# Adapter factors split into float32r parts of 64 rows, and the value bias joined to the output projection's row

## The chip, the cores and the metric

The kernel runs on one core of one Trainium2 chip. The metric is device time in microseconds (us) of one execution. The engines are named as the profile names them: PE is TensorE (matmuls; PEld is its weight load), DVE is VectorE, ACT is ScalarE, POOL is GpSimd, and SP only issues DMA transfers. "Bank" is one PSUM bank of 128 partitions x 512 float32 values, which is what one 128x512 matmul fills.

## The reference

x is float32 of 8 batches x 512 tokens x 512 features. It goes through four sublayers, each followed by a layer norm over the features:

```python
x = layernorm(x + attn0(x))   # 16 heads of 32, causal, biases on Q, K, V, O
x = layernorm(x + moe(x))     # 8 experts, top 2, adapters of rank 16
x = layernorm(x + attn1(x))   # grouped queries, 8 heads on 2
x = layernorm(x + ffn(x))     # SwiGLU on integer weights
```

The change touches the first two:

```python
q, k, v = x @ WQ.T + WQ_b, x @ WK.T + WK_b, x @ WV.T + WV_b     # per head of 32
attn = softmax(causal(q k^T / sqrt(32)))
attn0 = (attn @ v) @ WO.T + WO_b

router = xf @ gate.T + xf @ (2 * B @ A).T ; softmax ; top 2, renormalised
gup = xf @ gate_up[e] + 2 * (xf @ gup_A[e].T) @ gup_B[e].T      # 512 -> 512, A: 16 x 512
h   = silu(gup[:256]) * gup[256:]
out = h @ down[e] + 2 * (h @ down_A[e].T) @ down_B[e].T         # 256 -> 512, A: 16 x 256
moe = sum over the two chosen experts of weight * out
```

The rows of a softmax sum to 1, so a bias on v passes through the attention unchanged: `attn @ (v + bv) = attn @ v + bv`.

## The kernel before, in words

**Stages.** Attention of layer 0 runs from 0 to about 744 us, the experts to about 1160, attention of layer 1 to about 1750, and the integer feed-forward network to the end at 2309. Attention 0 works through 8 batches of about 94 us. Each batch has 4 groups g of 4 heads, and each group 3 units u of the keys' tiles (tile 0; tiles 1 and 3; tile 2), so there are 12 slots (g, u) to a batch. A slot makes its scores (`sc`, L1256), which ACT turns into `p` by an exponential (L1260) and POOL masks with an affine select (L1265). Then come the slot's other jobs, a list called `todo`, and then the products of the slot before (`av`, L1280), whose `p` VectorE adds up (L1288). In slot (g+1, 1) the group before is normalised: the sums over keys `rs` (L1295), ACT's copy `r_inv` of them, the reciprocal on VectorE (L1298, 3.34 us), and `aoT` (L1299).

**The order.** The block runs under `in_order`, which fixes TensorE's order to that of the text; the instructions of the other engines are placed by a scheduler that respects it. Every engine runs its own queue in order and waits on semaphores. The jobs in a slot are the values of the next batch (`value`, L1185, `ps_v`), the queries and keys of the next group (L1192, L1200), the output projection of the batch before (`project`, L1208), its transposes (`turn`), the router's logits (`score`) and choice (`choose`), and a `merge`.

**The adapters.** The adapters are not applied to tokens; the product of their factors is added to the experts' weights. For each pair of experts and each of 6 column blocks c a `merge` makes two products of 128x512 (`delta`, L749, factors of 16 rows in float32), ACT scales each by 2 into a tile `scaled` (L760) and POOL adds it into the expert's weights (L762). There are 24 merges. Two are done in each of batches 1 to 6, in slots (2, 0) and (3, 0); two stand after batch 7, and ten among the first expert steps. The factors of four experts are loaded by `load_lora` (L744) at the start, those of the other four in batch 7, 16 rows of 1792 values at partitions 0, 32, 64 and 96.

**Rings and banks that tie things together.** All jobs' matmuls use the PSUM tag `mm`, which has two banks; `sc` has one buffer of four banks. The SBUF tag `r_inv` has two buffers, which the normaliser's `r_inv` and the merge's `scaled` take in turn: a new user waits until the last reader of the one before is done, and for `scaled` that is POOL's add (L762), for `r_inv` POOL's add into `g_total` (L934). The `row` tile holds two rows broadcast over the partitions: WV's bias, added to each `ps_v` by VectorE (L1187), and WO's, added by POOL to the whole x of a batch (L1374) ahead of its projection. `first_turned` rooms of the first expert steps reuse the places of `row` and `logits` when attention is done.

**The tail.** When the last batch has gone through, expert steps begin (`tiles.step`: a tile's gate and up matmuls L845, the transposes of the step before, the down matmuls L862, and the fetch and transposes of later rows). Between them stand the last batch's transposes, logits, choice and dispatch, and one merge to a step.

Of the kernel before, what the change touches and what calls it, by code (L numbers as in the profile page):

```python
# [18 lines left out]
P = 128  # L19
NB = 8  # L20
S = 512
# [24 lines left out]
LORA = 3 * 512 + 256  # L46
EXPERT = UPS * 512
# [6 lines left out]
V_BQ, V_BK, V_NS, V_SS, V_SG, V_SU = 0, 4, 8, 12, 16, 16 + NHID  # L54
N_VEC = 16 + 2 * NHID
# [17 lines left out]
class Env:  # L73
# [53 lines left out]
    def load_adapters(self, pool):  # L127
        nc, ins = self.nc, self.ins
        self.lora_sb = pool.tile([P, 2, LORA], F32, name="lora_sb")
        for i in range(2):  # L130
            for j in range(4):
                nc.sync.dma_start(out=self.lora_sb[32 * j : 32 * j + R, i, :], in_=ins.lora[i, j])
        self.wr = pool.tile([P, ND, E], F32, name="wr")
        nc.sync.dma_start(out=self.wr, in_=ins.w_router)
        self.ra = pool.tile([R, D], F32, name="ra")
        nc.sync.dma_start(out=self.ra, in_=ins.router_lora_a)
        self.rb = pool.tile([R, E], F32, name="rb")
        nc.sync.dma_start(out=self.rb, in_=ins.router_lora_b)
# [246 lines left out]
class Router:  # L385
# [4 lines left out]
    def __init__(self, env, keep, pool, small, tmp, dram):  # L390
# [37 lines left out]
        i = tmp.tile([P, 1], I32, name="r_lane_i")  # L428
# [290 lines left out]
class Experts:  # L719
# [20 lines left out]
    def load_lora(self, pool, i):  # L740

        self.lora = pool.tile([P, LORA], F32, tag="lora", name=f"lora_{i}")
        for j in range(4):
            self.nc.sync.dma_start(out=self.lora[32 * j : 32 * j + R, :], in_=self.env.ins.lora[i, j])  # L744

    def delta(self, ps, e, c):
        j = 32 * (e % 4)
        a, bt = lora_factors(self.lora[j : j + R, :], c)
        self.nc.tensor.matmul(ps, lhsT=a, rhs=bt, start=True, stop=True)  # L749
# [15 lines left out]
class Tiles:  # L765
# [115 lines left out]
    def step(self):  # L881
        i = self.next
        self.next += 1
        if i + 1 < self.n:
            self.gate_up(i + 1, lambda: self.turn_hidden(i))
        else:
            self.turn_hidden(i)
        for n in range(4 if i == 0 else 5, 6):
            self.fetch(i + n)
        self.down(i)  # L890
        self.turn_rows(i + 3)
# [222 lines left out]
def attention0(env, guard, keep, routes, experts, dram, p_mm, tiles_ctx):  # L1114
# [8 lines left out]
    with ExitStack() as phase:  # L1123
# [33 lines left out]
        row = work.tile([P, 2, D], F32, name="row")  # L1157
        nc.sync.dma_start(out=row, in_=ins.rows.partition_broadcast(P))
# [9 lines left out]
        experts.load_lora(work, 0)  # L1168
# [13 lines left out]
        def value(b, t):  # L1182
# [4 lines left out]
            nc.vector.tensor_tensor(vs[t], ps, row[:, 0, :], ALU.add)  # L1187
# [122 lines left out]
        def plan(b):  # L1310
# [22 lines left out]
            if b == 0:  # L1333
                todo[1, 0].append(lambda: router.merge_lora(mm([P, ND, E], "ps_wr")))
            if b > 1:
                todo[0, 2].append(lambda: dispatch(b - 2))
                todo[1, 1].append(lambda: enter(one_hot(b - 2, range(NT))))
# [14 lines left out]
        def begin():  # L1352
            pair = work.tile([P, 2, D], F32, tag="row", name="first_turned")
            one = work.tile([P, S], F32, tag="logits", name="first_turned")
            tiles.begin([pair[:, 0, :], pair[:, 1, :], one], work.tile([P, 256], F32, name="first_h"),
# [11 lines left out]
        for b in range(NB):  # L1367
            todo = plan(b)
            for g in range(ND):
                if g == 2:  # L1370
# [3 lines left out]
                    nc.gpsimd.tensor_tensor(xs[b], xs[b], row[:, 1:2, :].to_broadcast([P, NT, D]), ALU.add)  # L1374
                if g == 3 and b + 1 < NB:
                    load_x(b + 1)
                if b == NB - 1 and g == 1:
                    experts.load_lora(work, 1)
# [36 lines left out]
        for c in range(ND):  # L1415
            turn(b, c)
        tiles.step()
# [6 lines left out]
        for places in ((0, 1), (2, 3)):  # L1424
            rows = one_hot(b, places)
            tiles.step()
            merge()
        enter(rows)
        tiles.of_fixed = router.fixed(routes)
        while merges:  # L1430
            tiles.step()
# [519 lines left out]
def _layout(a):  # L1951
# [26 lines left out]
    def columns(n):  # L1978
# [3 lines left out]
                           rows("L0_ffn_down_lora_A")], axis=3)  # L1982
    return {
# [5 lines left out]
                                  "L1_ffn_s_gate", "L1_ffn_s_up")], axis=1),  # L1989
# [29 lines left out]
```

## Time and profile before

| | us |
|---|---|
| median of 4 runs | 2311.31 (2307.61 to 2314.86) |
| the profiled execution | 2316.82 |
| its span | 2315.1 |
| PE busy | 2267.3 |
| DVE / ACT / POOL busy | 1238.9 / 654.2 / 502.1 |
| mean granted clock of TensorE | 0.994 |

The span is the time from the first instruction to the last of the profiled execution. A part of the profile that is used below is the timeline: a line gives the start in us, the duration in us, the engine, the source line and operation, the tiles (out <- in), the shape as partitions x elements, and the number of records that the line joins; in brackets stands the idle time of the engine just before it and what ended that idle time. A float32 matmul of 128x512 leaves two records and a float32r matmul one. A second view gives windows of time: the window, its length, the busy time of TensorE in it with the number of instructions, the clock that the throttle granted (1.00 is full speed), the share of DMA time, and GB/s.

Longest waits of TensorE, in all, from the view of waits (us in total, times, longest):

```
PE sc L1256 <- ACT p L1260: 5.2, 7, 1.8
PE ps_v L1185 <- DVE v L1187: 4.6, 5, 1.4
PE ps_q L1192 <- DMA experts<-in_xT: 4.4, 1, 4.4
PE ps_lora L749 <- DVE first_h L848: 2.9, 1, 2.9
```

The five waits for `v` stand at the start of batches 2 to 6, and the waits of `sc` for `p` behind the merge of slot (2, 0) in batches 1 to 6.

### The profile page before, as it was taken

The page shows a single profiled execution, that of the slowest core. Times are in us where ns is not written, and L with a number is a line of the kernel's source. Part 1 is how long each engine was busy: PE and PEld are TensorE (multiplying, and loading weights), DVE is VectorE, ACT ScalarE, POOL GpSimd, SP SyncE. Part 2 cuts the span into 40 slices and gives each one's busy share as a digit, 9 for nine tenths or more (in the row PEclk, how much of TensorE's full clock was granted, in tenths as well). Part 3 has the DMA queues.
Part 4 walks back from the last instruction along what each step waited for, and adds up shares of the span by engine and source line. Part 5 has one row for each costly group of instructions (what it writes and reads, how often), then busy time and mean ns, then how long its engine had stood idle before and what let it go on. Part 6 is the DMA issues. An engine that isn't in the chain of part 4 may idle for free.

```text
span 2315.1 us, 24139 instructions
## 1 busy us (share of the span) xinstructions
PE 2267.3 (98%) x9430; PEld 1140.8 (49%) x9430; DVE 1238.9 (54%) x1976; ACT 654.2 (28%) x937; POOL 502.1 (22%) x489
## 2 busy tenths in 40 slices
PE   9999999999998999999999999999999999999997
PEld 3344444444443444444543333333333777877776
DVE  3557565666667432232236776667666544444443
ACT  2332332323323221111223333333232222222222
POOL 2231423423324231221123222331211000000000
PEclk9999999999999999999999999999999999999999
DMA  8010110101112243332242011110100100000000
GB/s 286 19 55 1 55 49 7 55 19 37 54 37 87 87 140 124 106 109 91 87 156 63 15 40 55 55 36 19 37 1 1 54 19 19 19 19 19 19 19 20
DMA packets 58443, 126.62 MB, mean 55 GB/s; under 512 B 6210, under 2 KB 6210, under 8 KB 58322
## 3 DMA queue, kind: packets, MB, share of 16 engines
q1 hardware_dynamic: 47040, 89.32, 10.9%
q0 software_dynamic: 10560, 34.61, 5.1%
q8 instruction: 77, 1.26, 0.2%
q10 hardware_dynamic: 722, 1.07, 0.1%
q14 instruction: 44, 0.36, 0.1%
HBM read 89.59 MB, written 35.39 MB: 54 GB/s over the span
## 4 chain that ended last, share of the span: by engine, by line
PE 85%; DVE 8%; issue 2%; DMA 2%; POOL 2%; ACT 1%; POOLq 0%; SPq 0%; DVEq 0%; ACTq 0%
PE ps_gu L845 10%; PE ps_f L1061 7%; PE ps_g L1047 6%; PE ps_u L1047 6%; PE sc L1571 5%; PE av L1591 5%; PE ps_q L1495 5%; PE ps_o L1208 5%; PE ps_y L862 5%; PE ps_o L1543 5%; PE ps_q L1192 4%; PE ps_k L1200 4%; PE ps_v L1185 3%; PE av L1280 3%; PE sc L1256 3%
## 5 line engine op out<-in xcount | busy, mean ns | idle before, releaser
L845 PE MATMUL ps_gu<-experts,xrT 128*128 128x512 f32 (+1 forms) x520 | 247.2, 598 | 0.0
L1260 ACT ACTIVATE p<-sc 128x2048 f32<-128x2048 f32 (+1 forms) x96 | 152.9, 1593 | 189.0 <-PE sc L1256 182.1
L1574 ACT ACTIVATE p<-sc 128x1024 f32<-128x1024 f32 x128 | 131.0, 1024 | 256.2 <-PE sc L1571 243.8
L934 POOL TENSOR_TENSOR g_total<-g_total,r_inv 128x512 f32<-128x512 f32 x64 | 89.7, 1401 | 413.6 <-DVE r_inv L1602 338.2
L1265 POOL TENSOR_SCALAR_AFFINE_SELECT p<-p 128x512 f32<-128x512 f32 x128 | 93.0, 741 | 378.5 <-ACT p L1260 374.9
L1052 DVE SCALAR_TENSOR_TENSOR hT<-ps_u,vec,sg 128x512 f32<-128x512 f32 x88 | 65.9, 748 | 203.5 <-PE ps_u L1047 203.5
L1061 PE MATMUL ps_f<-ffn_w,h_half 128*128 128x512 f32 x672 | 169.7, 393 | 1.2 <-DVE h_half L1056 1.1
L1602 DVE RECIPROCAL r_inv<-r_inv 128x512 f32<-128x512 f32 x32 | 107.3, 3352 | 117.6 <-ACT r_inv L931 117.6
L1288 DVE TENSOR_TENSOR p<-p 128x1536 f32<-128x1536 f32 (+2 forms) x96 | 129.3, 1346 | 41.2 <-POOL p L1265 24.2
L1571 PE MATMUL sc<-qT,kT 64*128 64x512 f32 x512 | 144.2, 641 | 0.7 <-ACT qT L1497 0.7
L1047 PE MATMUL ps_g<-x_high,ffn_w 128*128 128x512 f32 x352 | 141.4, 402 | 3.0 <-DVE x L1549 3.0
L1582 DVE TENSOR_TENSOR p<-p,p 128x1024 f32<-128x1024 f32 x96 | 126.2, 1315 | 28.7 <-PE av L1591 13.9
L1061 PEld LDWEIGHTS ps_f<-ffn_w,h_half 128*128 128x128 f32 x672 | 124.5, 188 | 34.0 <-DVE h_half L1056 7.2
L1047 PE MATMUL ps_g<-x_low,ffn_w 128*128 128x512 f32 x352 | 139.8, 397 | 0.0
L1047 PE MATMUL ps_u<-x_low,ffn_w 128*128 128x512 f32 x352 | 139.5, 396 | 0.0
L1047 PE MATMUL ps_u<-x_high,ffn_w 128*128 128x512 f32 x352 | 139.4, 396 | 0.0
L848 DVE TENSOR_TENSOR h<-ps_gu,h 128x256 f32<-128x256 f32 x67 | 28.4, 423 | 206.5 <-ACT h L847 206.5
L1591 PE MATMUL av<-p,v 128*64 128x512 f32 x512 | 138.0, 617 | 0.2 <-ACT p L1574 0.2
L862 PE MATMUL ps_y<-experts,hT 128*128 128x512 f32 (+1 forms) x272 | 127.9, 592 | 0.5 <-ACT hT L856 0.5
L1192 PE MATMUL ps_q<-experts 128*128 128x512 f32 x256 | 120.2, 611 | 4.4 <-DMA experts<-in_xT 4.4
L845 PEld LDWEIGHTS ps_gu<-experts,xrT 128*128 128x128 f32 x520 | 89.1, 191 | 67.7 <-issue 67.7
L1185 PE MATMUL ps_v<-experts 128*128 128x512 f32 x256 | 116.3, 602 | 4.6 <-DVE v L1187 4.6
(255 smaller groups left out, 3517.2 us busy)
## 6 DMA issues: line engine op xcount, KB each, us to landing
results<-y SPq DMA_DIRECT2D x68, 256.0 KB, 2.0
x<-in_x SPq DMA_DIRECT2D x8, 1024.0 KB, 8.0
experts<-in_gate_up SPq DMA_DIRECT2D x8, 1024.0 KB, 11.8
rows<-x SPq DMA_DIRECT2D x32, 256.0 KB, 2.0
x<-rows SPq DMA_DIRECT2D x8, 1024.0 KB, 11.1
experts<-in_xT SPq DMA_DIRECT2D x7, 1024.0 KB, 5.4
out<-x SPq DMA_DIRECT2D x28, 256.0 KB, 2.3
ffn_i<-in_wq_ffn SPq DMA_DIRECT2D x11, 512.0 KB, 4.2
```

The lines of the kernel that those rows point to most:

```text
L845: mm = nc.tensor.matmul(ps, lhsT=xT[:, c, :], rhs=self.weights(i, c), start=c == 0, stop=c == ND - 1)
L862: self.nc.tensor.matmul(ps, lhsT=hT[:, c, :], rhs=self.weights(i, ND + c), start=c == 0, stop=c == self.NI - 1)
L1047: nc.tensor.matmul(ps, lhsT=w[:, ts(dc, P)], rhs=x[:, dc, :], start=(dc, i) == (0, 0), stop=(dc, i) == (ND - 1, 1))
L1061: self.nc.tensor.matmul(os[t], lhsT=h[:, ts(t, P)], rhs=self.weights(2 * NHID + c), start=(c, i) == (0, 0), stop=(c, i) == (NHID - 1, 1))
L1185: nc.tensor.matmul(ps, lhsT=xts[b][:, c, ts(t, P)], rhs=wv[:, c, :], start=c == 0, stop=c == ND - 1)
L1192: nc.tensor.matmul(ps, lhsT=wq[:, g, ts(c, P)], rhs=xts[b][:, c, :], start=c == 0, stop=c == ND - 1)
L1260: nc.scalar.activation(p, sc[:, :, :width], AF.Exp, scale=scale)
L1288: nc.vector.tensor_tensor(total[:, :, P * kt :], total[:, :, P * kt :], p[:, :, at : at + w], ALU.add)
L1571: nc.tensor.matmul(sc[:, j, :], lhsT=st["kT"][hs, ts(kt, P)], rhs=st["qT"][g][hs, :], start=True, stop=True)
L1574: nc.scalar.activation(p, sc, AF.Exp, scale=scale)
L1582: nc.vector.tensor_tensor(total, total, p, ALU.add)
L1591: nc.tensor.matmul(st["av"][HD * j : HD * (j + 1), :], lhsT=st["v"][:, kt, HD * j : HD * (j + 1)], rhs=p[:, j, :], start=kt == 0, stop=kt ...
```

## The change

Adapters. On the host each factor row is repeated: a pair of experts has 128 rows, 64 for each expert, which are its 16 rows four times over. The kernel fetches a pair in four parts of 512, 512, 512 and 256 columns into one tile `l_raw`, and splits each part. `l_high` is the raw value rounded to float32r, with its sign turned in some of the four copies. `lora` is `raw * low + high` with `low` 0 or 1, which is the rounded value in one set of copies and what rounding leaves of it in the other. The two factors of a product have these copies in different order, so that the sum over 64 rows holds high x high, high x low, low x high and low x low, and one float32r matmul of 64 rows stands for the float32 matmul of 16.

```diff
+    def masks(self, pool, lane):
+        bits = pool.tile([P, 2], I32, name="l_bits")
+        self.low = pool.tile([P, 2], F32, name="l_low")
+        self.sign = pool.tile([P, 2], F32, name="l_sign")
+        for i, bit in enumerate((2 * R, R)):
+            nc.vector.tensor_scalar(bits[:, i : i + 1], lane, bit, None, ALU.bitwise_and)
+        nc.vector.tensor_copy(self.low, bits)
+        nc.vector.tensor_scalar(self.low, self.low, 1.0, None, ALU.min)
+        nc.vector.tensor_scalar(self.sign, self.low, -2.0, 1.0, ALU.mult, ALU.add)
+        self.parts = [(q, c) for q in range(E // 2) for c in range(LORA_PARTS)]
+
+    def fetch_part(self, pool):
+        if self.parts:
+            q, c = self.parts[0]
+            at, n = 512 * c, min(512, LORA - 512 * c)
+            self.raw = pool.tile([P, 512], F32, tag="raw", name="l_raw")
+            self.nc.sync.dma_start(out=self.raw[:, :n], in_=self.env.ins.lora[q, :, at : at + n])
+
+    def split_part(self, pool):
+        q, c = self.parts.pop(0)
+        if c == 0:
+            self.lora = pool.tile([P, LORA], F32R, tag="lora", name=f"lora_{q}")
+        at, n = 512 * c, min(512, LORA - 512 * c)
+        i = int(c in (1, 2))
+        high = pool.tile([P, 512], F32R, tag="r_inv", name="l_high", bufs=2)[:, :n]
+        nc.scalar.activation(high, self.raw[:, :n], AF.Copy, scale=self.sign[:, i : i + 1])
+        nc.vector.scalar_tensor_tensor(self.lora[:, at : at + n], self.raw[:, :n], self.low[:, i : i + 1],
+                                       high.bitcast(F32), ALU.mult, ALU.add)
+        if (q, c) != (E // 2 - 2, LORA_PARTS - 1):
+            self.fetch_part(pool)

     def delta(self, ps, e, c):
-        j = 32 * (e % 4)
-        a, bt = lora_factors(self.lora[j : j + R, :], c)
+        j = P // 2 * (e % 2)
+        a, bt = lora_factors(self.lora[j : j + P // 2, :], c)
         self.nc.tensor.matmul(ps, lhsT=a, rhs=bt, start=True, stop=True)
```

The sixteen splits are placed in slots: four in batch 0, two each in batches 3, 4, 6 and 7, and four among the expert steps. The next part is fetched as soon as a split is issued, and needs the one `raw` buffer, so it waits for that split. `load_lora` at the start and in batch 7 falls away. In the tail two merges move from the steps between the one-hot rows to the last steps, which take two merges each.

```diff
+            slots = {0: ((2, 0), (2, 2), (3, 0), (3, 2)), 3: ((3, 1), (3, 2)), 4: ((1, 1), (1, 2)),
+                     6: ((3, 1), (3, 2)), 7: ((0, 1), (1, 1))}
+            for slot in slots.get(b, ()):
+                todo[slot].append(lambda: experts.split_part(work))
...
         for places in ((0, 1), (2, 3)):
             rows = one_hot(b, places)
+            experts.split_part(work)
             tiles.step()
-            merge()
+            experts.split_part(work)
         enter(rows)
         tiles.of_fixed = router.fixed(routes)
         while merges:
-            tiles.step()
+            tiles.step(merge)
             merge()
```

`tiles.step` takes a function `amid`, which it calls ahead of the down matmuls.

Bias. The values are evacuated without a bias, even tiles by a copy on VectorE, odd ones by a copy on ACT. A job `join_bias` in slot (1, 2) of batch 0 multiplies WV's bias by the output projection's weights (four float32 matmuls of 128x512) and adds the product to WO's bias in `row`, which now holds one row.

```diff
             vs[t] = own.tile([P, D], F32, tag=f"v{t}", name=f"v{t}")
-            nc.vector.tensor_tensor(vs[t], ps, row[:, 0, :], ALU.add)
+            env.evacuate(t, vs[t], ps)
+
+        def join_bias():
+            bv = work.tile([P, ND, P], F32, tag="r_inv", name="bv", bufs=2)
+            nc.vector.tensor_copy(bv, vec[:, V_BV : V_BV + ND, None].to_broadcast([P, ND, P]))
+            ps = mm([P, D], "ps_bias")
+            for c in range(ND):
+                nc.tensor.matmul(ps, lhsT=bv[:, c, :], rhs=wo[:, c, :], start=c == 0, stop=c == ND - 1)
+            nc.vector.tensor_tensor(row, ps, row, ALU.add)
...
-                    nc.gpsimd.tensor_tensor(xs[b], xs[b], row[:, 1:2, :].to_broadcast([P, NT, D]), ALU.add)
+                    nc.gpsimd.tensor_tensor(xs[b], xs[b], row[:, None, :].to_broadcast([P, NT, D]), ALU.add)
```

The rooms of the first expert steps are now the places of `row`, `logits` and `raw`.

## The prediction

> **What bounds the kernel now.** I read the page's first and second parts first, then the chain that ended last, then TensorE's order of work and its waits at the twelve places that the change touches.
>
> ```profile
> span 2315.1 us, 24139 instructions
> ...
> PE 2267.3 (98%) x9430; PEld 1140.8 (49%) x9430; DVE 1238.9 (54%) x1976; ACT 654.2 (28%) x937; POOL 502.1 (22%) x489
> ```
>
> TensorE is busy for 98% of the span and no other engine for more than 54%. An edit pays only by TensorE's own time, and costs by what it adds there or by making TensorE wait. TensorE's order is fixed, so a wait is not filled by other work. In batch 0, TensorE then POOL:
>
> ```profile
> 49.93 3.70 PE L1200 MATMUL ps_k<-experts 128*128 128x512 f32 x8
> 53.56 1.07 PE L1280 MATMUL av<-p,v 128*32 128x384 f32 x16
> ...
> 61.53 1.06 PE L1280 MATMUL av<-p,v 128*32 128x512 f32 x8 [0.36 <-POOL p L1265]
> ```
>
> ```profile
> 53.83 1.59 POOL L934 TENSOR_TENSOR g_total<-g_total,r_inv 128x512 f32<-128x512 f32 x1 [2.04 <-DVE r_inv L1298]
> 55.38 5.51 POOL L1374 TENSOR_TENSOR x<-x,row 128x2048 f32<-128x2048 f32 x1
> 60.83 1.82 POOL L1265 TENSOR_SCALAR_AFFINE_SELECT p<-p 128x512 f32<-128x512 f32 x3
> ```
>
> The add of the row to x already stands ahead of the select that av waits for (0.36). At the end of batch 3, TensorE, then POOL:
>
> ```profile
> 353.93 1.04 PE L1295 MATMUL rs<-p,ones 128*32 128x512 f32 x8
> ...
> 370.85 3.70 PE L1185 MATMUL ps_v<-experts 128*128 128x512 f32 x8 [0.82 <-DVE v L1187]
> ```
>
> ```profile
> 350.08 4.54 POOL L1374 TENSOR_TENSOR x<-x,row 128x2048 f32<-128x2048 f32 x1 [3.28 <-DMA x<-in_x]
> 354.58 2.50 POOL L762 TENSOR_TENSOR experts<-experts,scaled 128x512 f32<-128x512 f32 x2
> ```
>
> The adapters' adds end at 357.08 because POOL waits for x. In the stage of the experts, two steps with a pair of products and one without:
>
> ```profile
> 834.57 1.13 PE L749 MATMUL ps_lora<-lora 16*128 16x512 f32 x4
> 835.63 1.98 PE L845 MATMUL ps_gu<-experts,xrT 128*128 128x512 f32 x4
> ...
> 842.69 1.98 PE L845 MATMUL ps_gu<-experts,xrT 128*128 128x512 f32 x4
> ...
> 861.70 1.88 PE L845 MATMUL ps_gu<-experts,xrT 128*128 128x512 f32 x4
> ...
> 867.51 1.88 PE L845 MATMUL ps_gu<-experts,xrT 128*128 128x512 f32 x4
> ```
>
> A step takes 7.06 with the pair (842.69 - 835.63) and 5.81 without: a pair costs 1.25.
>
> **The shorter products.** A float32 matmul of 128x512 is two records; four matmuls take 3.43 (0.858 each). A float32r one starts every 0.2335 (FFN: 1899.86, 1900.09, 1900.33). The old pair's four records start two by two (834.571 and .578, 835.105 and .111): the two experts already run side by side. The second two follow after 0.534, where half a float32 matmul is 0.429: about 0.1 is switching. So I take 0.2335 + 0.1 = 0.33 for the new pair in place of 1.06, which saves about 0.75. Bounds: 0.85 if switching vanishes, 0.5 if the 64-row products don't run side by side (2 x 0.2335 + 0.1 = 0.57).
>
> Twelve pairs lie in batches 1 to 6 and gain nothing. After slot (2,0)'s pair TensorE waits 0.57 for the exponential (421.13); that ends when it ended before, so the wait grows to about 1.2. After slot (3,0) what is gained (up to 0.85) is waited off at ps_v (0.44 to 1.40 at five batch starts): the wait ends a chain that begins with the landing of x, goes through the row add on POOL and the adapters' adds, and ends in VectorE's routing work. That the even copies of v stay on VectorE keeps this wait.
>
> The two pairs at the end of batch 7 (734.20 to 742.74) run at half clock, around a wait of 2.89 for first_h, which stays. I take 3.0 off: 1.06 of serial time at the second pair, the 0.73 wait behind it shortened by some 0.2, one half-clock window of 3.41 fewer (1.7). Bounds 1 and 4.
>
> Ten pairs stand between 773.95 and 848.70: 10 x 0.75 = 7.5, less 0.28 where ps_r at 794.02 waits for the logits' copy anyway, plus 0.74: ps_table (819.86) no longer stands behind a pair's scaling. That is 8.0. Six of these pairs now go two to a step. POOL's four adds then take 4 x 1.3 of a step of some 6.5 us and cover themselves, with about half a microsecond in hand; without that cover ACT's scaling, and the SiLU and hT behind it, would be late by the difference. The half-clock window at 803.39 follows one with 2.68 busy; with less waiting ahead of it I take half of its 1.7 as gone, 0.9.
>
> **The bias, in batch 0.** TensorE gains four float32 matmuls, 3.43, after ps_k. They need bv, which VectorE makes after the reciprocal that ends at 53.8: 0.68 (as a copy of a 128x512 bank) makes it 54.4, so TensorE waits 0.87. VectorE then makes aoT (0.68), two adds of p, one split, and the row at about 58.7. POOL in the new order adds the row to x of batch 0 and then of batch 1, 2 x 4.51, before the select (0.64) that av of slot (2,0) needs: 58.7 + 9.0 + 0.7 = 68.45. That av ran at 61.53. Cost 6.9, of which 4.3 are the bias and its wait and 2.9 a new stall, with 0.36 of wait it replaces. With 5.51 for one add (as at 55.38) it is 7.9. Bound below: 4.3, if the adds are hidden. In return value() loses nothing on TensorE: v's addition (0.683) becomes a copy of 0.683, half of them on ACT.
>
> **The splits.** No operation in the trace rounds with a per-row scale from SBUF. Nearest rows: ACT's cast of h_half, 0.62, and VectorE's scalar_tensor_tensor of a bank, 0.75. Sixteen of each and sixteen fetches (12 of 256 KB, 4 of 128 KB; rows of 256 KB land in 2.0, at the start up to 4.0) replace eight fetches that landed in 6.7. SP issues them after existing requests; x and xT wait behind a raw fetch only where that waits for the preceding split, and there x is due more than 10 us later.
>
> Where they stand in the queues matters more. In batch 0 the third rounding waits for its fetch ahead of an exponential: 0.85 (0 to 1.7). In batch 3 the rounding stands on ACT behind the two scalings and takes a ring buffer that POOL's first adapter add frees at 354.58 + 1.25 = 355.83. Then rounding (356.45), VectorE's split (357.2), and behind it in VectorE's queue the query's bias (0.75, 358.0), whose PSUM bank rs needs: rs goes from 353.93 to 358.05, +4.1. The 0.82 wait at 370.85 then vanishes: +3.3. In batch 6 the same chain starts from POOL's add at 634.82 + 1.25: rs from 635.99 to 638.2, +2.2, with no wait behind it to give back. Bounds: 0 for both if ACT's rounding does not hold VectorE; 1 us more each if an operation is twice its row. The other splits (batches 4 and 7, the last four among the expert steps) stand beside TensorE work with over 1 us of margin: 0.
>
> **The clock.** After a stretch with little work TensorE runs at half speed for a 3.41 us window, which costs 1.7:
>
> ```profile
> 1219.80:1223.23 3.43, 1.11 (x8) 1.00 0.00 1
> 1223.23:1226.64 3.41, 3.41 (x7) 0.50 0.02 5
> ...
> 718.06:721.47 3.41, 1.92 (x28) 1.00 0.81 303
> ```
>
> 2.32 idle drew a half-speed window, 1.49 did not. Setting the edge at 1.9 and the window's phase at random, a stall of 2.9 falls into one window deeply enough in 74 of 100 (1.3), of 4.1 always (1.7), of 2.2 in 53 of 100 (0.9): 3.9 in all, bounds 0 and 8. The Trainium skill ("TensorE: Matmul & The Clock Gate", section "HAM oscillation — how this bites in real kernels") says that gaps beyond about 3.4 us are what must be avoided. By it only the 4.1 would pay, and the sum would be 2.2 lower. The row at 1219.80 shows that a shorter one is enough, so I keep mine.
>
> **The sum.** Added: 6.9 + 0.85 + 3.3 + 2.2 + 3.9 = 17.15. Removed: 3.0 + 8.0 + 0.9 = 11.9. Net +5.25. The profiled execution took 2316.82 (span 2315.1 and 1.7 around it), which becomes 2322.1; it lies 5.5 over the median 2311.31 of the four runs. On that median: 2316.6.
>
> **Rivals.**
> B, slower still: the stalls multiply half-clock windows. Each of the three draws two windows instead of the 3.9 counted together: 3 x 2 x 1.7 - 3.9 = +6.3, so 2323; with slower splits 2325. For it: the long half-speed stretch of 10.24 at 738.54, after 2.89 of idle. Against: at 1223 and 1796 one window was enough. It decides from two further windows.
> C, faster: TensorE does not wait for the splits. If rs in batches 3 and 6 stays where it was and the select in batch 0 is not held by the two adds, only 4.3 for the bias and 0.85 remain against 11.9: 2304.6, or 2303.7 without the 0.85. For it: ACT is busy only 28%, and ACT and VectorE have idle time of 2 to 8 us around these places. Against: the queues are in order, and the waits named stand in them. It needs all three stalls gone.
> D, the products do not run side by side (64 rows each, in another mode than their neighbours): 10 x 0.25 = 2.5 less: 2319. For it: no float32r pair stands in this trace. Against: the 16-row pair does it. The skill speaks against the change here ("TensorEngine Tiling (Array Packing)", section "Key Properties"): a change of the tiling mode drains TensorE, which the 16-row pairs pay as well; by it the 0.1 is not smaller for 64 rows.
>
> **How the numbers follow.** 0.3% of 2311.31 is 6.9, about what a measurement of this kernel can tell from no change: faster is below 2304.4, slower above 2318.2. The forecast gets 0.50, with its own range 2311 to 2322 and a third of it above 2318.2; B 0.25, C 0.15, D 0.10. Slower: 0.17 + 0.25 + 0.07 = 0.49; faster: nearly all of C, 0.14; same 0.37. Range: from C at 2303 to just over B, 2327.
>
> **What would show it.** Right: TensorE waiting at av near 68 us for POOL's p, and at rs near 360 and 645 for VectorE's q; the wait behind slot (2,0)'s pair grown to 1.2; a step with two pairs near 6.5 (5.81 + 2 x 0.5 is 6.8 at most); half-speed windows behind the three stalls. Wrong: rs without waits, a pair over 0.6, or a stall at the tail's hT for ACT's scaling, or more than 4.3 lost in attention outside batches 0, 3 and 6.

## The result, and the profile after

The changed kernel takes 2315.35 us (median of 32 runs, 2312.6 to 2320.82), the kernel before 2312.32 on the same chips (52 runs, 2307.15 to 2317.27). The ratio is 1.0017 [1.0012, 1.0022]: 3.0 us slower by the two medians and 3.9 by the ratio. That is clear of 1, but smaller than the 0.3% that the prediction set as its bound for a change.

The profiled execution of the changed kernel is a quick one: 2312.23, or 3.1 below its median, where that of before (2316.82) lies 4.5 above the median of the 52. So the spans compare the wrong way round, and only a comparison place by place tells what happened. Of the page, span and busy time:

```profile
span 2310.5 us, 24139 instructions
...
PE 2254.4 (98%) x9390; PEld 1137.5 (49%) x9390; DVE 1241.3 (54%) x1983; ACT 672.6 (29%) x969; POOL 496.4 (21%) x489
```

TensorE is busy for 12.9 less than before, and VectorE and ACT for 2.4 and 18.4 more (the splits, and on ACT half of the copies of v). The view of TensorE's waits (total, times, longest) shows what took part of that back:

```profile
PE sc L1301 <- ACT p L1305: 9.0, 8, 1.8
PE rs L1340 <- DVE q L1239: 6.7, 2, 4.3
...
PE av L1325 <- POOL p L1310: 2.9, 1, 2.9
...
PE ps_v L1221 <- DVE v L164: 2.0, 2, 1.0
```

The waits of `rs` and of `av` are new. The waits of `sc` for `p` grew from 5.2 in all to 9.0: the six behind the merge of slot (2, 0) went from 0.57 or 0.58 to 1.00 each, one of 1.21 in batch 0 is new, and that of 1.8 at the end of batch 7 stayed. Three of the five waits of `ps_v` are absent.

**Batch 0.** The timeline of the changed kernel, the lines that follow the bias:

```profile
54.50 0.35 DVE L1228 COPY bv<-vec 128x512 f32<-128x512 f32 x1
...
54.95 3.67 PE L1231 MATMUL ps_bias<-experts,bv 128*128 128x512 f32 x8 [0.49 <-issue]
...
58.66 0.69 DVE L1232 TENSOR_TENSOR row<-ps_bias,row 128x512 f32<-128x512 f32 x1
...
59.44 9.00 POOL L1424 TENSOR_TENSOR x<-x,row 128x2048 f32<-128x2048 f32 x2 [3.46 <-DVE row L1232]
...
68.38 1.82 POOL L1310 TENSOR_SCALAR_AFFINE_SELECT p<-p 128x512 f32<-128x512 f32 x3
69.07 1.06 PE L1325 MATMUL av<-p,v 128*32 128x512 f32 x8 [2.90 <-POOL p L1310]
```

Read it downwards: the four bias matmuls end at 58.6, VectorE makes the row, POOL adds it to two batches of x for 9.00, only then selects, and `av` has stood for 2.90. A little later the third rounding waits for its fetch, the exponential stands behind it, and `sc` waits for that:

```profile
78.50 0.72 ACT L773 ACTIVATE l_high<-l_raw,l_sign 128x512 fp32r<-128x512 f32 x1 [2.50 <-DMA l_raw<-in_lora]
...
81.04 1.15 PE L1301 MATMUL sc<-q,k 32*128 32x384 f32 x16 [1.21 <-ACT p L1305]
```

**Batch 3.** The same chain as before, with the splits in it:

```profile
358.25 4.52 POOL L1424 TENSOR_TENSOR x<-x,row 128x2048 f32<-128x2048 f32 x1 [3.27 <-DMA x<-in_x]
...
362.73 2.48 POOL L796 TENSOR_TENSOR experts<-experts,scaled 128x512 f32<-128x512 f32 x2
364.02 0.72 ACT L773 ACTIVATE l_high<-l_raw,l_sign 128x512 fp32r<-128x512 f32 x1 [7.68 <-POOL experts L796]
...
364.78 0.98 DVE L774 SCALAR_TENSOR_TENSOR lora<-l_raw,l_low,l_high 128x512 fp32r<-128x512 f32 x1 [12.94 <-ACT l_high L773]
365.69 0.74 DVE L1239 TENSOR_SCALAR q<-ps_q,vec 128x512 f32<-128x512 f32 x1
...
366.48 1.94 PE L1340 MATMUL rs<-p,ones 128*32 128x512 f32 x8 [4.33 <-DVE q L1239]
```

The chain starts on POOL: it adds the row to x ahead of the adapter's add, and for that waits for x. ACT's rounding needs the buffer that the adapter's add frees, VectorE's split stands in its queue behind the rounding, and the query's bias behind the split. `rs` comes last and waits 4.33.

**The experts.** The last steps, each from one `ps_gu` to the second next:

```profile
830.40 0.49 PE L783 MATMUL ps_lora<-lora 64*128 64x512 f32 x2
830.83 1.98 PE L879 MATMUL ps_gu<-experts,xrT 128*128 128x512 f32 x4
...
834.68 0.50 PE L783 MATMUL ps_lora<-lora 64*128 64x512 f32 x2
835.11 1.98 PE L896 MATMUL ps_y<-experts,hT 128*128 128x512 f32 x4
...
837.90 1.98 PE L879 MATMUL ps_gu<-experts,xrT 128*128 128x512 f32 x4
```

A step with two pairs takes 7.07 (837.90 - 830.83), one without 5.81: 0.63 for a pair, where it was 1.25. The pair itself takes 0.43 (830.83 - 830.40), its two matmuls side by side.

The two profiles against each other, by the start of the same matmul in both; "predicted" is the prediction's terms for that place:

| place | predicted | after less before |
|---|---|---|
| start, before the change can act | 0 | +0.8 |
| batch 0 (bias, select, exponential, clock) | +9.1 | +8.0 |
| batches 1, 2 | 0 | -0.6 |
| batch 3 (`rs`, clock) | +5.0 | +5.9 |
| batches 4, 5 | 0 | -1.8 |
| batch 6 (`rs`, clock) | +3.1 | +4.0 |
| batch 7 | 0 | +1.1 |
| the two pairs behind batch 7 | -3.0 | -7.8 |
| ten pairs among the steps | -8.9 | -8.6 |
| rest of the experts | 0 | -0.5 |
| attention 1 | 0 | -2.3 |
| feed-forward | 0 | -2.9 |
| end | 0 | 0.0 |
| sum, before rounding | +5.3 | -4.6 |

Two rows hold chance beside the change. In attention 1 no instruction differs; this profile of the kernel before has a window at half speed at 1223 behind a wait of 2.32 at `rs`, and that of the changed kernel has a wait of 1.69 there and no such window. Among the twelve profiles of the runs below, two have that window, one of the kernel before and one of the changed. The two pairs behind batch 7 are taken up below.

### The profile page after: what moved, and what is told of

It reads as the page before. It is cut to its first block, busy times and chain, and to the rows that moved or that the text cites. A ratio compares the mean times of both kernels' runs of the same rounds, so it can differ in the third digit from the quotient of the medians.

```text
span 2310.5 us, 24139 instructions
## 1 busy us (share of the span) xinstructions
PE 2254.4 (98%) x9390; PEld 1137.5 (49%) x9390; DVE 1241.3 (54%) x1983; ACT 672.6 (29%) x969; POOL 496.4 (21%) x489
## 4 chain that ended last, share of the span: by engine, by line
PE 87%; DVE 6%; issue 2%; POOL 2%; DMA 2%; ACT 1%; POOLq 0%; SPq 0%; DVEq 0%; ACTq 0%
PE ps_gu L879 9%; PE ps_f L1096 7%; PE ps_g L1082 6%; PE ps_u L1082 6%; PE sc L1622 6%; PE av L1642 5%; PE ps_q L1546 5%; PE ps_o L1253 5%; PE ps_y L896 5%; PE ps_o L1594 5%; PE ps_k L1245 4%; PE ps_v L1221 4%; PE ps_q L1237 4%; PE sc L1301 3%; PE av L1325 3%
## 5 line engine op out<-in xcount | busy, mean ns | idle before, releaser
L1245 PE MATMUL ps_k<-experts 128*128 128x512 f32 x256 | 119.5, 610 | 0.2 <-ACT r_inv L966 0.2
```

The costliest lines, as they stand in the source:

```text
L1245: nc.tensor.matmul(ps, lhsT=wk[:, g, ts(c, P)], rhs=xts[b][:, c, :], start=c == 0, stop=c == ND - 1)
```

## The experiments

Ratios are to the kernel before, measured beside each run, with 95% intervals. Differences to the changed kernel are to its median of 2315.35, which was not measured beside each of them; the medians of the kernel before lay between 2311.41 and 2312.95, so such a difference is good to about 1 us.

**Without the bias' product.** The job is not placed; WV's bias is left out.

```diff
-            if b == 0:
-                todo[1, 2].append(join_bias)
```

> The changed kernel without the job that joins the value bias to the row, so the bias of WV is left out of the output altogether; the values are still evacuated by copies. If the bias costs what the sum said (four matmuls and their wait 4.3, the stall behind the row's adds 2.9, an exponential that came 1.2 late after it, some half-speed windows), this is 7 to 9 us faster than the changed kernel: about 2308, ratio to before 0.998, with no wait of TensorE at av near 69 us and the group sums of batch 0's second group back at 62 to 63. Rival: the matmuls hide in TensorE's other waits and the cost is the copies of v; then it gains under 2 us.

2308.44, ratio 0.9984 [0.9975, 0.9994]: 6.9 below the changed kernel. `av` at slot (2, 0) of batch 0 waits for nothing, and `rs` behind it stands at 61.80 instead of 69.96. The bias costs its matmuls and the stall at the select, as the theory has it. The late exponential is not the bias' doing: `sc` still waits for it, 1.59.

**The splits in other slots.** Those of batch 3 go to batch 4, those of batch 6 to batch 7.

```diff
-            slots = {0: ((2, 0), (2, 2), (3, 0), (3, 2)), 3: ((3, 1), (3, 2)), 4: ((1, 1), (1, 2)),
-                     6: ((3, 1), (3, 2)), 7: ((0, 1), (1, 1))}
+            slots = {0: ((2, 0), (2, 2), (3, 0), (3, 2)), 4: ((0, 0), (0, 2), (1, 1), (1, 2)),
+                     7: ((0, 0), (0, 2), (1, 0), (1, 1))}
```

> The changed kernel with the two splits of batch 3 moved to slots (0,0) and (0,2) of batch 4, and the splits of batches 6 and 7 to slots (0,0), (0,2), (1,0), (1,1) of batch 7. If the waits at rs (4.33 and 2.37) come from a rounding that waits on ACT for POOL's adapter add, they vanish, the wait for v at batch 4's start comes back (0.8 to 1.4), and three half-speed windows (1.7 each) with them: 6 to 9 us faster than the changed kernel, about 2308, ratio to before 0.998. Rival: a split costs the same wherever it stands, since it holds ACT and VectorE; then new waits of 2 to 4 us appear in batches 4 and 7 and the time stays near 2315.

2306.12, ratio 0.9976 [0.9966, 0.9986]: 9.2 below the changed kernel. Both waits of `rs` are gone, and so are the half-speed windows behind them. The wait that they had hidden is back, in the timeline of this run:

```profile
380.81 3.70 PE L1221 MATMUL ps_v<-experts 128*128 128x512 f32 x8 [1.44 <-DVE v L164]
```

**The products in float32.** The same factors of 64 rows, the same splits.

```diff
-        self.nc.tensor.matmul(ps, lhsT=a, rhs=bt, start=True, stop=True)
+        self.nc.tensor.matmul(ps, lhsT=a.bitcast(F32), rhs=bt.bitcast(F32), start=True, stop=True)
```

> The changed kernel with the same 64-row factors multiplied in float32 (four passes) in place of float32r; all else stays, the splits and the order too. If the gain is in the shorter products, a pair takes 1.06 again in place of 0.43: ten pairs among the expert steps cost 6.3 more, the two pairs behind batch 7 one to three more, and the pairs in batches 1 to 6 nothing, since TensorE waits there anyway (the wait of sc for the exponential falls from 1.0 to 0.4 to 0.6): 7 to 10 us slower than the changed kernel, about 2323, ratio to before 1.005. Rival: the gain in the tail comes from the new order of the merges; then it is under 2 us slower.

2322.57, ratio 1.0041 [1.0026, 1.0057]: 7.2 above the changed kernel. The timeline of this run:

```profile
836.04 1.13 PE L783 MATMUL ps_lora<-lora 64*128 64x512 f32 x4
837.10 1.98 PE L879 MATMUL ps_gu<-experts,xrT 128*128 128x512 f32 x4
...
845.42 1.98 PE L879 MATMUL ps_gu<-experts,xrT 128*128 128x512 f32 x4
```

A step with two pairs takes 8.32, so a pair costs 1.255, what it cost with 16 rows: a pair's own gain is the float32r pass, and 64 rows are as cheap as 16. It is not all of the 8.6 won on the ten pairs, though. The half-speed window at 803 and the wait of `ps_table` (0.74) of the kernel before are absent here too, with float32 products; ten pairs at 0.63 more give back 6.3, and some 2.3 stay. The wait behind slot (2, 0) shrinks to 0.37 here: in batches 1 to 6 the time saved on a pair is indeed waited off.

**One merge to a step.** Undoes the pairing of merges in the tail.

```diff
-            tiles.step(merge)
+            tiles.step()
```

> The changed kernel with its last six merges one to a step in place of two. Theory: what the tail gained is the products' own time, so this is within 1 us of the changed kernel. Rival 1: two to a step is itself a gain; then 2 us or more slower. Rival 2: two to a step makes ACT's scaling late for SiLU and hT; then faster by 1 to 3 us.

2315.40, ratio 1.0013 [1.0004, 1.0022], the time of the changed kernel. A step with one pair takes 6.44, again 0.63 for the pair: where the pairs stand is worth nothing.

This run tells something else. Up to the last six merges it is the changed kernel, instruction for instruction, yet in its profile the same stretch behind batch 7 runs otherwise. The view of windows (window, length, busy time of the engines with their instructions, TensorE's clock, DMA share, GB/s), first of the changed kernel, then of this one:

```profile
738.00:770.00 32.00, 29.04 (x137) 13.10 (x138) 28.91 (x69) 10.69 (x18) 13.14 (x13) 0.95 0.11 34
```

```profile
738.00:770.00 32.00, 28.47 (x128) 12.64 (x129) 28.27 (x69) 11.51 (x18) 13.27 (x13) 0.84 0.13 43
```

A mean clock of 0.95 is 3.41 at half speed, 0.84 is 10.24. This run stands 0.78 behind the changed kernel ahead of the stretch (`sc` at 738.88 and 738.10) and 3.51 behind it (`ps_o` at 765.72 and 762.21): 2.7 lost in the same code, with the same waits ahead of the stretch. The profile of before has 10.24 at half speed there too. So of the 6.7 that batch 7 and the two pairs behind it gain together in the table (+1.1 and -7.8), 2.7 is the luck of one execution, and 4.0 is left.

Nor are those 4.0 all the change's. In the kernel before the second expert's product of the first pair waits for `first_h`; in the kernel before with another order on POOL (a run below), whose products are the old ones, it does not:

```profile
738.21 1.80 PE L749 MATMUL ps_lora<-lora 16*128 16x512 f32 x4 [2.89 <-DVE first_h L848]
```

```profile
731.43 4.07 PE L749 MATMUL ps_lora<-lora 16*128 16x512 f32 x8
```

What goes with the wait is the clock ahead of it. In 12 of the 14 profiles a half-speed window begins within 3 us behind the `sc` at the end of batch 7 that waits for `p` (738.10 in the changed kernel), TensorE comes to the first `ps_gu` of the experts 8.8 to 9.9 after that `sc`, and nothing waits for `first_h`. In the other two, of the kernel before and of the same with a wider `vec`, no such window stands there, `ps_gu` comes after 7.4, and the wait is 2.89. From that `sc` to `ps_o` it is 30.8 in the kernel before, 28.7 in the one with the other order on POOL (13.65 at half speed) and 26.4 to 26.8 in the six profiles of changed code with 10.24 at half speed. So of the 4.0 (30.8 less 26.8 in this run) 1.8 is left against an execution without the wait (28.7), and its one more half-speed window (1.7) makes up nearly all of that.

**The row's add later on POOL.** In the changed kernel POOL adds the row to x of a batch wherever the scheduler puts it. Here it waits until the last select of slot (1, 2) of that batch has been issued; `selects` is a list to which every select is appended.

```diff
+                    with tc.issue_after(selects[-1].ins):
                         nc.gpsimd.tensor_tensor(xs[b], xs[b], row[:, None, :].to_broadcast([P, NT, D]), ALU.add)
```

> The changed kernel with POOL's add of the row to x held behind the last select of slot (1,2) of its own batch, so that it never stands ahead of the adapters' adds of slot (3,0) while it waits for x from memory, and batch 1's add does not follow batch 0's. Theory: the stall at av (2.9), both waits at rs (4.33, 2.37) and the waits for v at the starts of batches 2 and 5 (2.0) all go back to this add, with three or more half-speed windows behind them: 10 to 15 us faster than the changed kernel, about 2303, ratio to before 0.996. Rival 1: the rounding's place on ACT is enough to hold rs; then only the 2.9 and the 2.0 go, about 2310. Rival 2: the add at its new place holds back the select of slot (2,0) in every batch (4.5 us of work ahead of it), and TensorE waits at av in batches 1 to 7: no gain or slower.

2307.12, ratio 0.9979 [0.9971, 0.9988]: 8.2 below the changed kernel, short of what the theory wanted. The waits of `av`, `rs` and `ps_v` are all gone, but batches 1, 2, 3, 5 and 6 have a new one of 0.73 and one of 0.44 in slots (1, x), and batch 4 has one of 1.65 with a half-speed window behind it. The same two adds of `p`, in the timeline of this run, where POOL's add of the row runs from 135.97 to 140.49, and of the changed kernel, where it does not run beside them:

```profile
138.04 5.21 DVE L1335 TENSOR_TENSOR p<-p 128x512 f32<-128x512 f32 x2
```

```profile
141.83 2.86 DVE L1333 TENSOR_TENSOR p<-p 128x512 f32<-128x512 f32 x2
```

They overlap POOL's add by 2.45 and last 2.35 longer. The Trainium skill ("SBUF — State Buffer", section "Who interferes with whom") says that a VectorE instruction with two inputs in SBUF contends with a GpSimd one that reads SBUF, for a port pair that only one of them holds at a time; these rows agree, since VectorE loses about the whole overlap.

**The adapters' adds first.** The row's add of batches 2 to 7 stands behind the adapters' last add in POOL's queue; batches 0 and 1 are left as they are.

```diff
-            self.nc.gpsimd.tensor_tensor(w, w, scaled[i], ALU.add)
+            self.added = self.nc.gpsimd.tensor_tensor(w, w, scaled[i], ALU.add)
...
+                    with tc.issue_after(experts.added.ins) if b > 1 else nullcontext():
                         nc.gpsimd.tensor_tensor(xs[b], xs[b], row[:, None, :].to_broadcast([P, NT, D]), ALU.add)
```

> The changed kernel with one order changed on POOL: in batches 2 to 7 the add of the row to x is held behind the adapters' adds of the slot before it, so that these no longer wait for x from memory. Nothing else moves: the splits stay in their slots and the rounding in its place on ACT. Theory: the waits at rs in batches 3 and 6 (4.33 and 2.37) and the waits for v (2.0 in two batches) vanish, with up to three half-speed windows (1.7 each): 7 to 11 us faster than the changed kernel, about 2306. The stall at av near 69 us stays. Rival: the rounding and the split themselves hold rs by their own time, some 1 to 2 us of waits at rs stay in both batches, and the row's add, now later, holds the selects of slot (3,1): about 2311.

2303.55, ratio 0.9957 [0.9944, 0.9969]: 11.8 below the changed kernel. The timeline of this run in batch 3, to be read against the one above:

```profile
354.61 2.51 POOL L796 TENSOR_TENSOR experts<-experts,scaled 128x512 f32<-128x512 f32 x2 [0.35 <-ACT scaled L794]
...
355.92 0.72 ACT L773 ACTIVATE l_high<-l_raw,l_sign 128x512 fp32r<-128x512 f32 x1 [0.30 <-POOL experts L796]
...
357.69 4.54 POOL L1425 TENSOR_TENSOR x<-x,row 128x2048 f32<-128x2048 f32 x1 [0.57 <-DVE lora L774]
...
361.24 1.04 PE L1340 MATMUL rs<-p,ones 128*32 128x512 f32 x8
```

The rounding starts at 355.92, 8.1 earlier, and `rs` waits for nothing. With the split where the change put it, only POOL's order is different, and the stall is gone. The run with the splits in other slots left POOL's order and lost the stall too: it takes both, the row's add ahead of the adapter's and a split that stands behind that in these slots. The `ps_v` waits are gone too.

**The same, and batches 0 and 1 behind the select.**

```diff
-                    with tc.issue_after(experts.added.ins) if b > 1 else nullcontext():
+                    with tc.issue_after((experts.added if b > 1 else selects[-1]).ins):
```

> The kernel with the adapters' adds first, and beside that the row's adds of batches 0 and 1 held behind the last select of slot (1,2) of their own batch, so that batch 1's add doesn't follow batch 0's ahead of the select that av needs. Theory: the stall of 2.9 at av near 69 us goes too, and 3 us come off the kernel with the adapters' adds first alone: about 2303, ratio to before 0.996. Rival: batch 1's add holds back something in batch 1 as long (a select, or VectorE's work on x), and the two are equal.

2297.64 (2296.47 to 2298.66), ratio 0.9935 [0.9922, 0.9948]: the shortest that computes all of the reference, 17.7 below the changed kernel and 15.3 below the kernel before (2312.95 beside it). It is 5.9 below the run above, where the theory had 3. The stall at `av` (2.9) is gone; two waits in batch 1 (0.72 and 0.45) are new, as in the run with the row's add later. Up to the end of the feed-forward network's matmuls the profile has 6.83 at half speed where that of the run above has 13.65, which is another 3.4 between these two executions.

**The kernel before with the same order of POOL.** Does the order, rather than the change, make that?

```diff
+                    with tc.issue_after(experts.added.ins) if b > 1 else nullcontext():
                         nc.gpsimd.tensor_tensor(xs[b], xs[b], row[:, 1:2, :].to_broadcast([P, NT, D]), ALU.add)
```

> The kernel before with the same order on POOL, and nothing of the change: the adapters' adds ahead of the row's add in batches 2 to 7. Theory: the waits for v at the starts of batches 2 to 6 (4.6 in all) end a chain behind the landing of x and the adapters' adds, so they vanish: 4 to 5 us faster than before, ratio 0.998. Rival: they end VectorE's routing work alone; then no change.

2309.05, ratio 0.9983 [0.9974, 0.9991]: 3.9 below the kernel before, with the five waits of `ps_v` (4.6) all gone. With this order on POOL in both, the change is worth 5.5 (2309.05 - 2303.55). Holding back the adds of batches 0 and 1 as well makes it 11.4 (2309.05 - 2297.64), of which the stall at `av` merely takes back what the bias had brought.

**Batch 1's row add pulled forward.** It goes behind the last select of batch 0, to take the two new waits away.

```diff
-                    with tc.issue_after((experts.added if b > 1 else selects[-1]).ins):
+                    with tc.issue_after((experts.added if b > 1 else selects[15] if b else selects[-1]).ins):
```

> The kernel with the adapters' adds first and both early row adds held back, where batch 1's row add now stands behind the last select of batch 0 and no longer beside batch 1's projections. Theory: the two waits that came with its place in batch 1 (0.72 at the pair's bank and 0.45 at the first transpose, both for VectorE's work on x) vanish, so it is about 1.2 us faster than that kernel: about 2296.5, ratio to before 0.993. Rival: they are the layer norm's own chain; then equal, 2297.6.

2298.43, ratio 0.9944 [0.9931, 0.9958]: not told apart from 0.9935. The two waits (1.17) are gone, but behind batch 7 the profile has 10.24 at half speed where the other has 3.41. Whether the one causes the other was not settled.

**The same without the bias' product** (WV's bias is left out; the edit is that of the first run).

> The same kernel with both row adds held back and early, without the job that joins the value bias, so the bias of WV is left out of the output. Theory: with the stall behind the row's adds gone, what the bias still costs is TensorE's own four matmuls and the wait ahead of them, 3.4 + 0.5: about 4 us faster than with it, about 2292.5. Rival: the four matmuls stand in a place where TensorE would wait for the late exponential of slot (3,0) anyway; then 2 us or less.

2293.50, ratio 0.9921 [0.9908, 0.9934]: 4.9 below the run above. With its stall removed, the bias' product still costs its four float32 matmuls and the wait ahead of them. Its return, a copy instead of an add on VectorE, shows in no wait of TensorE. A product in float32r for the bias was not tried.

**The feed-forward network.** The 2.9 gained there are in a stage that the change doesn't touch. What differs is an address: the tile `vec` grew from 38 to 42 columns for the bias, and the tiles that are laid out behind it, among them the feed-forward network's halves of x, its hidden halves and its later weights, moved by 32 bytes. The kernel before, with `vec` wider by as much and no instruction changed:

```diff
-        self.vec = const.tile([P, N_VEC], F32, name="vec")
+        self.vec = const.tile([P, N_VEC + 4], F32, name="vec")
...
-        nc.scalar.dma_start(out=self.vec, in_=ins.vecs)
+        nc.scalar.dma_start(out=self.vec[:, :N_VEC], in_=ins.vecs)
```

> The kernel before with the tile of column vectors allocated 4 columns wider and no instruction changed, so that the tiles behind it, the feed-forward network's halves of x, hidden halves and later weights among them, lie 32 bytes further on, at addresses of 32 modulo 64, as they do in the changed kernel. Theory: the 2.9 us by which the last stage is shorter in every kernel with the change (502.4 us from its first float32r matmul to the last, against 505.3) come from this place in memory, so this stage falls to 502.4 and the kernel is about 3 us faster than before: ratio 0.9987. Rival: they come from what ran before (the adapters' parts, another state of the clock or of a queue); then the stage stays at 505.3 and the time is that of before.

And the changed kernel with `vec` wider by 8 columns, which puts those tiles back to a multiple of 64 bytes from where they were:

```diff
+        self.vec = const.tile([P, N_VEC + 8], F32, name="vec")
```

> The changed kernel with the same tile another 8 columns wider and no instruction changed, so that these tiles lie at 0 modulo 64 again, as before the change. Theory: its last stage goes back to 505.3 us and the kernel is about 3 us slower than the changed one, 2318, ratio to before 1.0027 or so. Rival: the stage stays at 502.4 and the time at 2315.

The first takes 2309.42, ratio 0.9988 [0.9979, 0.9997] (2.4 faster); the second 2320.86, ratio 1.0040 [1.0027, 1.0054], 5.5 above the changed kernel. First and last block of the stage (it begins at 1795 and not at about 1750) in the timelines, kernel before, then with `vec` wider:

```profile
1795.43 0.50 PE L1047 MATMUL ps_g<-x_high,ffn_w 128*128 128x512 f32 x1 [3.00 <-DVE x L1549]
...
2295.97 7.41 PE L1061 MATMUL ps_f<-ffn_w,h_late 128*128 128x512 f32 x32
```

```profile
1797.63 0.50 PE L1047 MATMUL ps_g<-x_high,ffn_w 128*128 128x512 f32 x1 [3.00 <-DVE x L1549]
...
2295.20 7.41 PE L1061 MATMUL ps_f<-ffn_w,h_late 128*128 128x512 f32 x32
```

500.54 and 497.57. The changed kernel has 497.68, and 502.15 when shifted back: in both kernels the 32 bytes are worth 3 to 4.5. The other runs agree: of all 14 profiles the three with these tiles at a multiple of 64 bytes have 500.54, 500.63 and 502.15, ten of the rest 497.23 to 497.88, and the one with float32 products 498.93, with 6.14 at half speed in the stage. Half speed does not make the difference: 502.15 and 497.23 both have none of it in the stage. The groups of the two kernels before show where, here one of the four kinds of product, which lost 4 ns of 396 in each matmul:

```profile
L1047 PE MATMUL ps_u<-x_low,ffn_w 128*128 128x512 f32 x352 | 139.5, 396 | 0.0
```

```profile
L1047 PE MATMUL ps_u<-x_low,ffn_w 128*128 128x512 f32 x352 | 138.0, 392 | 0.0
```

Which tile's address does it was not told apart.

## Why the prediction was right, and where it was not

The predicted 2316.6 lies 1.3 above the median, and the time is in the range. As a difference, though, 5.25 was forecast and 3.0 measured. Of the closeness 1.0 is luck of the four runs that it was added to (median 2311.31, against 2312.32 over 52), and one gain was missing from the working (below).

**The bias: right.** 6.9 was predicted for it, and `rs` of batch 0 came 6.7 later, beyond the 0.8 of the start; removing it gave 6.9. The wait ahead of the matmuls is 0.49, not 0.87, because VectorE makes `bv` in 0.35 (its source is in SBUF; the row that I took for it copies a PSUM bank). The stall of 2.90 is the 2.9 of the working. The third rounding waits for its fetch as forecast, and `sc` behind it for 1.21 where 0.85 was counted.

**The splits in batches 3 and 6: right, with the reason one step short.** Predicted were delays of 4.1 and 2.2, measured are waits of 4.33 and 2.37; the difference is the split, 0.98 instead of 0.75. The working named the chain that starts at POOL's row add, but treated that order as given. The run with the adapters' adds first shows that the stall hangs on it: 11.8 in all for an edit to POOL's queue alone.

**The wait for v: half right.** The one at batch 4's start went, as predicted. Those at the starts of batches 2 and 5 (0.44 and 1.40) are absent too, which was not; 1.6 of the 1.8 won over batches 4 and 5 falls at the latter. But that is this execution's: with the same instructions up to there, batch 2 waits 0.52 in the run with one merge to a step, and batches 2 and 5 wait 0.49 and 0.98 in the changed kernel shifted back. So these waits are no steady gain of the change.

**The pairs: the mechanism right, the size off.** The step "I take 0.2335 + 0.1 = 0.33 for the new pair" failed: the pair takes 0.43. The ten pairs then give 0.62 each, not 0.75, and the statement that a step with two pairs takes "6.8 at most" failed with it, since it left out the switching on both sides of a pair, which stays: 0.63 - 0.43 = 0.20, for 64 rows as for 16 (1.25 - 1.06 = 0.19). The half-speed window at 803 went fully (1.7), where half of it was counted, so that the place gave 8.6 where 8.9 was predicted. The reason given for it, less waiting ahead, is not what took it: it is absent with float32 products too, and from all 11 profiles with 64 rows, while each of the three with 16 rows has one or two between 795 and 807. Rival D (2.5 lost) would have a pair of 0.57; it fell.

**Batches 1 to 6: right.** The wait behind slot (2, 0) went from 0.57 to 1.00 (1.2 was forecast) and took the gain, and the float32 products took it back to 0.37.

**Behind batch 7: the sign right, the size not.** 3.0 was predicted, with one half-speed window fewer in it; by the repeat of the same code 4.0 is gained against the kernel before with as many at half speed as there, and 1.8 against the execution of the old products without the wait. The two pairs did not both run at half clock in the kernel before, as the working has it: its half speed starts at 738.5, behind the wait, and the first half of the first pair stands ahead of it at 734.20. The step "the wait of 2.89 for first_h, which stays" failed: in both runs nothing waits for `first_h`, and the pair waits 0.75 for ACT's scaling of the one before.

```profile
752.08 0.50 PE L783 MATMUL ps_lora<-lora 64*128 64x512 f32 x1
753.32 0.77 PE L783 MATMUL ps_lora<-lora 64*128 64x512 f32 x2 [0.75 <-ACT scaled L794]
```

By the 14 profiles it is not the change that removes the wait: it comes and goes with the half-speed window ahead of it. That the slower TensorE lets VectorE get ahead fits this; no run tests it.

**The clock: right in the sum, wrong in the places.** 1.3 + 1.7 + 0.9 was predicted for three stalls. Batch 0's drew no half-speed window, batch 3's drew two and batch 6's one: 5.1 against 3.9. The windows of the changed kernel, around the three:

```profile
64.41:67.83 3.42, 1.76 (x4) 0.46 (x3) 0.75 (x1) 1.85 (x1) 3.42 (x1) 1.00 0.00 0
67.83:71.24 3.41, 2.17 (x20) 0.73 (x24) 0.96 (x1) 0.17 (x1) 2.36 (x4) 1.00 0.00 0
361.37:364.78 3.41, 0.78 (x8) 0.00 (x0) 0.00 (x1) 0.76 (x2) 3.41 (x3) 1.00 0.00 0
364.78:368.20 3.42, 1.72 (x8) 0.20 (x8) 2.88 (x5) 1.96 (x2) 1.65 (x3) 0.50 0.28 77
648.09:651.50 3.41, 1.04 (x12) 0.16 (x8) 1.98 (x5) 2.71 (x3) 2.04 (x4) 1.00 0.13 21
651.50:654.91 3.41, 3.41 (x15) 1.45 (x12) 3.41 (x3) 2.32 (x4) 0.94 (x2) 0.50 0.15 56
```

The stall of 2.90 lies across an edge: 1.66 idle in one window, 1.24 in the next, and the clock stays at 1.00. That of 2.37 lies in one window, and the next has 0.50. Here the phase decides, and the prediction could do no more than give it a chance. The Trainium skill ("TensorE: Matmul & The Clock Gate", section "HAM oscillation — how this bites in real kernels") names gaps beyond about 3.4 us. By that the stall of 2.37 would have cost nothing; the row at 651.50 shows half speed behind it.

**What was missing: the feed-forward network.** The working had 0 for every stage behind the experts, because no instruction changes there. It gave 2.9. Without it the changed kernel would be some 6 slower than before (3.0 + 2.9); the kernel shifted back, at 1.0040, says 9. So the rest of the working was short by 0.7 to 3.8 (by the profiles the clock, the pairs and the third rounding are among what it had too cheap), and a gain that it did not have covered that.

Rival B (three stalls with two windows each) had its mechanism in batch 3 alone. Rival C (no stalls) fell by the waits; with POOL's order mended it is the 2297.64, lower than the 2304.6 it was given.

## What to carry to other kernels

Before an operation is hung behind a buffer that another engine frees, follow that engine's queue to what its own head waits for: here the wait for x passed through POOL, ACT and VectorE to TensorE, and one line of order on POOL was worth 11.8 us, more than the 7.2 of the faster products. A saving counts only where nothing waits right behind it: of 24 pairs, the twelve in batches 1 to 6 gave nothing. When a change adds to a constant tile, compare the untouched stages too; an address may have moved.

## What the runs showed of the hardware

- The feed-forward matmuls depend on where their tiles lie in SBUF: 32 bytes of shift made the stage 497.57 instead of 500.54, and back 502.15 instead of 497.68, with the same instructions.
- VectorE's adds of two SBUF tiles lose about all the time that POOL's add runs beside them: 5.21 instead of 2.86 with 2.45 of overlap. Work moved on POOL therefore moves a cost on VectorE.
- For a half-speed window the idle time within one window of 3.41 us counts: 2.37 in one drew it, 2.90 split over two (1.66 and 1.24) did not. Idle time is not all: the half-speed window at 803.39 of the kernel before follows one with 2.67 busy. The same code lost 2.7 us more in one execution than in another, so that two single profiles can differ by more than the change.
